# FFT channels of two frequencies in three blocks of 128, two frequency groups, e5m2 transposes and another order of the first loads

## The chip, the cores and the metric

The kernel runs on one core of a Trainium2 chip. The core has five engines, each with a queue of its own that it works through in order: TensorE (PE in the profile, with PEld for its weight loads), VectorE (DVE), ScalarE (ACT), GpSimd (POOL) and SyncE (SP), which here issues all DMAs. The metric is the device time of one execution in microseconds; three runs of the kernel before gave 4522.43, 4522.75 and 4531.9, median 4522.75. The profile is of one further execution, of 4534.8 us by the same clock; the span of its trace is 4533.0 us.

## What is computed

An input of 32 images of 56 x 56 pixels and 96 channels goes through two layers.

- Layer 0 is a convolution block whose weights are mixed per image. The pooled image gives four gates, `rw = sigmoid(pooled @ Wr + br)`; they mix four sets of weights. A pointwise expansion takes 96 to 384 channels, a 3 x 3 depthwise convolution follows, and a pointwise projection takes 384 back to 96. Each has a batch norm, and the input is added.
- Layer 1, first half: every image is a sequence of 3136 tokens. After a layer norm, tokens are projected to 192 channels, and a Fourier transform runs along the 3136 tokens:

```python
h = jax.nn.relu(_bn(jnp.einsum('bnc,hc->bnh', x, w1), ...))
X = jnp.fft.fft(h, axis=1, norm='ortho')
xr = jax.nn.relu(X.real * rd - X.imag * idg + rb)
xi = jax.nn.relu(X.imag * rd + X.real * idg + ib)
y = jnp.fft.ifft(xr + 1j * xi, axis=1, norm='ortho').real
o = jnp.einsum('bnh,ch->bnc', y, w2)
```

  `rd` and `idg` are one number per channel, so the nonlinearity works on each channel and frequency alone.
- Layer 1, second half: layer norm, then two linear layers (96 to 384 to 96) whose operands are rounded to e5m2, an 8-bit float with 5 exponent and 2 mantissa bits.

## The kernel before

An image lies in SBUF as 96 channels by 3136 pixels (`xs[b]`, three buffers). The transform of length 3136 = 56 x 56 is done in two steps of matrix products, with a round trip through DRAM between them. By the names of the tiles:

- `expansion` (tiles `ps_pw`): PE makes 384 channels in three blocks `c` of 128, for each half `p` of the image; ACT evacuates with Relu into the padded tile `hp`. It waits for the mixed weights `wk` of the image. The half p = 1 is computed in 9 + 9 + 8 rows.
- `convolved_tensor` (`ps_dw`) and `convolved_vector` (tile `h`, nine steps): the depthwise convolution, some blocks as 32 x 32 diagonal products on PE, some on DVE.
- `projection` (`ps_pwl`), then `forward(parity)`: transposes and moments of a strip (`ps_t_a`), projection to 192 channels (`ps_w` on `w1c`, evacuated by DVE as `ha`), the first transform step (`ps_a`, evacuated by ACT as `g`), and a write to DRAM (`gd`).
- `frequency_loads` loads groups of the 29 first-step frequencies back into the tile `g2`, called `g` in the profile. `GROUPS` is four groups of 8, 7, 7, 7, and `g2` has two buffers.
- `frequencies` makes the second transform step (`ps_b`): for each group and each half `h` of the 192 channels, one product per frequency, with 96 channels as the stationary (loaded) operand and the 112-column matrix `dftb_s` moving. So the result has 96 channels on partitions.
- `nonlinearity` and `imaginary_parts` work on that result: ACT makes `zi`, `zr` and an absolute value, POOL adds, ACT does a Relu, DVE does four steps that read PSUM or SBUF (tiles `z`, `mir`).
- `spectrum` multiplies by `w2` (`ps_w` on `w_s` and `z`, two products for each frequency, one for each half), ACT copies out (`zo`), `ps_c` makes the first inverse step, DVE copies out, and `zo` goes to DRAM (`yd`).
- `inverse(parity)`: loads a strip `yt`, makes the last inverse step (`ps_d`), adds to the image, transposes (`ps_t_f`), takes moments, normalises on ACT in seven instructions of 96 columns, transposes back (`ps_n`, f32), and runs the two e5m2 layers (`ps_f`; `hidden` between them).

The order of all this is written by a planner when the program is built (class `Plan`). Each step is a generator that yields the engine it wants, the events it waits for and the buffers it takes. The planner keeps a clock per engine with a cost for each instruction (`Engine`, and `mm` for products) and always lets the stream go on that can start first; among equals the smaller priority number wins. The numbers stand in the list at the end of the kernel and in the calls of `plan.spawn`. All PSUM is four buffers of two banks (`ps=4`). When a step on PE gets its buffer and the planner's clock says that PE will stand idle, `psum` puts filler products into the gap, of the size 112 x 112 and at most 40; in the profile they are the lines with L320:

```python
for _ in range(min(40, int((plan.idle() - 0.3) / 0.19))):
    nc.tensor.matmul(ps[:PB, 0:PB], dftb_s, dftb_s, start=True, stop=True)
```

Because the queues are in order, the order that the planner writes is what the chip runs; an engine that is late makes those behind it late.

Ahead of the planned part stands a preparation: loads of all constants by SP, and some 70 small instructions, mostly on DVE, that fold batch norms into the weights. The image loads (`loads`) come after all constants. `mixing` then pools an image on DVE, makes the gates (`ps_rw`, then a sigmoid on ACT with its table load, then four DVE steps for `wk`).

Of the kernel before, what the change touches and what calls it, by code (L numbers as in the profile page):

```python
# [40 lines left out]
F32 = mybir.dt.float32  # L41
# [16 lines left out]
SP64 = 64  # L58
# [20 lines left out]
GROUPS = [(0, 8), (8, 7), (15, 7), (22, 7)]  # L79
# [206 lines left out]
def kernel(  # L286
# [20 lines left out]
    NB = x.shape[0]  # L307

# [14 lines left out]
    plan = None  # L323

# [7 lines left out]

    wpw_s = const([C, NE, M], F32, "wpw_s")
    nc.sync.dma_start(wpw_s, wpw)
    wr_s = const([C, NE], F32, "wr_s")
    nc.sync.dma_start(wr_s, wr)
# [3 lines left out]
    vec_s = const([128, NVECS], F32, "vec_s")  # L340
    nc.sync.dma_start(vec_s, vecs)
# [8 lines left out]
    w2_s = const([C, 2, C], F32, "w2_s")  # L350
    nc.sync.dma_start(w2_s, w2t)
# [11 lines left out]
    nc.vector.tensor_add(ident32, ident32, ident[:, 96:128])  # L363
    ones = const([C, 128], F32, "ones")
# [19 lines left out]
    nid = const([128, 2], F32, "nid")  # L384
    nrd = const([128, 2], F32, "nrd")
# [6 lines left out]
    with tc.tile_pool(name="prep", bufs=1) as pp:  # L392
        row_s = pp.tile([128, NROWS], F32, tag="row_s", name="row_s")
        nc.sync.dma_start(row_s, rows.partition_broadcast(128))

        def row(name, p=128):
            lo, hi = ROWS[name]
            return row_s[:p, lo:hi]

        def bn_scale(to, gamma, var, eps):  # L400

            nc.vector.tensor_scalar_add(to, var, eps)
            nc.scalar.activation(to, to, AF.Sqrt)
            nc.vector.reciprocal(to, to)
            nc.vector.tensor_mul(to, to, gamma)

        bn_scale(s1, vec("g1"), vec("v1"), EPS_CONV)
        bn_scale(s2, vec("g2"), vec("v2"), EPS_CONV)
        bn_scale(s3, vec("g3"), vec("v3"), EPS_CONV)
        bn_scale(sc, vec("cg"), vec("cv"), EPS_ATTN)  # L410
        s1row = pp.tile([C, M], F32, tag="s1row", name="s1row")
        bn_scale(s1row, row("g1", C), row("v1", C), EPS_CONV)
        s3row = pp.tile([128, C], F32, tag="s3row", name="s3row")
        bn_scale(s3row, row("g3"), row("v3"), EPS_CONV)
        sarow = pp.tile([128, CH], F32, tag="sarow", name="sarow")
        bn_scale(sarow, row("ag"), row("av"), EPS_ATTN)
        scrow = pp.tile([C, C], F32, tag="scrow", name="scrow")
        bn_scale(scrow, row("cg", C), row("cv", C), EPS_ATTN)


        for e in range(NE):
            nc.vector.tensor_mul(wpw_s[:, e, :], wpw_s[:, e, :], s1row)
            for c in range(NC3):
                nc.vector.tensor_mul(wpwl_s[:, e, c, :], wpwl_s[:, e, c, :], s3row)
        for h in range(2):
            nc.vector.tensor_mul(w2_s[:, h, :], w2_s[:, h, :], scrow)

        mean_m = pp.tile([C, C], F32, tag="mean_m", name="mean_m")
        nc.gpsimd.memset(mean_m, 1.0 / C)
        center_m = pp.tile([C, C], F32, tag="center_m", name="center_m")  # L430
        nc.vector.tensor_sub(center_m, ident[:C, :C], mean_m)
        nc.vector.tensor_mul(w1c, w1c, sarow[0:C, :])
        ps_c = psum("ps_w1c")
        nc.tensor.matmul(ps_c[:C, 0:CH], center_m, w1c, start=True, stop=True)
        nc.vector.tensor_copy(w1c, ps_c[:C, 0:CH])
        nc.vector.tensor_mul(nshift, row("am"), sarow)
        nc.vector.tensor_sub(nshift, nshift, row("ab"))

        ps_s = psum("ps_shift")
        for h in range(2):  # L440
            nc.tensor.matmul(
                ps_s[:C, 512 * h : 512 * h + 1],
                nshift[0:1, C * h : C * h + C],
                ones[0:1, 0:1],
                start=True,
                stop=True,
            )
        for h in range(2):
            for j, by in enumerate(("rd", "id")):
                nc.vector.scalar_tensor_tensor(  # L450
                    dc[:C, h, j : j + 1], ps_s[:C, 512 * h : 512 * h + 1], -float(S),
                    vec(by)[:C, h : h + 1], ALU.mult, ALU.mult,
                )


        for c in range(NC3):
            taps = stk_s[:, 9 * c : 9 * c + 9, 0:NE]
            nc.vector.tensor_scalar_mul(taps, taps, s2[:, c : c + 1])
            k = 9 * NC3 + c
            nc.vector.tensor_scalar_mul(stk_s[:, k, 0:NE], stk_s[:, k, 0:NE], s1[:, c : c + 1])  # L460
            k += NC3
            nc.vector.tensor_scalar_mul(stk_s[:, k, 0:NE], stk_s[:, k, 0:NE], s2[:, c : c + 1])
        nc.vector.tensor_scalar_mul(stk_s[:, NSTK - 1, 0:NE], stk_s[:, NSTK - 1, 0:NE], s3)
        nc.vector.memset(stk_s[:, 0 : 9 * NC3, NE : NE + 1], 0.0)

        def bn_shift(to, beta, mean, scale, tag):

            tmp = pp.tile(list(mean.shape), F32, tag=tag, name=tag)
            nc.vector.tensor_mul(tmp, mean, scale)
            nc.vector.tensor_sub(to, beta, tmp)  # L470

        k = 9 * NC3
        bn_shift(stk_s[:, k : k + NC3, NE], vec("b1"), vec("m1"), s1, "sh1")
        bn_shift(stk_s[:, k + NC3 : k + 2 * NC3, NE], vec("b2"), vec("m2"), s2, "sh2")
        bn_shift(stk_s[:, NSTK - 1 : NSTK, NE], vec("b3"), vec("m3"), s3, "sh3")
        bn_shift(cb, vec("cb"), vec("cm"), sc, "shc")
        nc.vector.tensor_scalar_mul(nid, vec("id"), -1.0)
        nc.vector.tensor_scalar_mul(nrd, vec("rd"), -1.0)
        nc.vector.tensor_copy(br_s, row("br"))
        for q in range(1, G):  # L480
            for to, at in turned(q):
                nc.sync.dma_start(
                    stk_s[to, NSTK + NPE * (q - 1) : NSTK + NPE * q, :],
                    stk_s[at, 10 * NC3 : 10 * NC3 + NPE, :],
                )


        f1 = pp.tile([C, M], F32, tag="f1", name="f1")
        nc.sync.dma_start(f1, fw1t)
        nc.vector.tensor_copy(fw1, f1, saturate=False)  # L490
        f2 = pp.tile([128, NC3, C], F32, tag="f2", name="f2")
        nc.sync.dma_start(f2, fw2t)
        nc.vector.tensor_copy(fw2, f2, saturate=False)
        q1 = pp.tile([128, NC3], E5M2, tag="q1", name="q1")
        nc.vector.tensor_copy(q1, vec("fb1"), saturate=False)
        nc.vector.tensor_copy(fb1, q1)
        q2 = pp.tile([128, 1], E5M2, tag="q2", name="q2")
        nc.vector.tensor_copy(q2, vec("fb2"), saturate=False)
        nc.vector.tensor_copy(fb2, q2)
# [9 lines left out]
    for t in hp:  # L509
        nc.gpsimd.memset(t, 0.0)  # L510

# [34 lines left out]
    mixed, small_of, wk2s, gds, yds, g2s, zs = {}, {}, {}, {}, {}, {}, {}  # L546


    def loads():
        for b in range(NB):  # L550
            yield SP, [("out", b - 3, s) for s in range(NS) if b >= 3]
            Q.dma_start(xs[b], x[b])
            arrives(4 * C * N, "x", b)
# [71 lines left out]
    def expansion():  # L625

        for b, p, before in parts_of_all():
            xb = xpad[b % 3]
            for c in (2, 0, 1):

                for part, (at, ns) in enumerate(((0, (9, 9)), (18, (8, 8) if p == 0 else (8,)))):
                    yield PE, [("wk", b)] + (readers(*before, c) if before else []), 1
                    wk = mixed[b]
                    ps = psum(f"ps_pw_{b}_{p}_{c}_{part}")
                    for j, n in enumerate(ns):
                        lo = (G * BW * p + at + j * n) * S
                        mm(
                            ps[:, 512 * j : 512 * j + n * S],
                            wk[:, 128 * c : 128 * c + 128],
                            xb[:, lo : lo + n * S],  # L640
                        )
                    plan.spawn("evac pw", 6, expanded(b, p, c, part, at, ns, ps))
# [17 lines left out]
    def convolved_tensor():  # L660

        for b, p, before in parts_of_all():
            for i, wave in enumerate(WAVES[p]):
# [24 lines left out]
                plan.spawn("evac dw", 3, convolved(b, p, i, wave, ps))  # L688
# [41 lines left out]
    def projection():  # L730

        for b, p, _ in parts_of_all():
            needs = [("h2t", b, p, i) for i in range(len(WAVES[p]))] + [("wk2", b)]
            needs += [("h2v", b, p, c) for c, *_ in ON_VECTOR[p]]
            for s, blocks in (((0, (0, 1)), (1, (2, 3))), ((2, (4, 5)), (3, (6,))))[p]:
# [13 lines left out]
                plan.spawn("evac prj", 0, projected(b, s, blocks, ps))  # L749
# [89 lines left out]
    def frequency_loads():  # L839
        n = 0  # L840
        for b in range(NB):
            for i, (k0, nk) in enumerate(GROUPS):
                yield SP, [("g", b, s) for s in range(NS)] + [("g2", n - 2)] * (n >= 2)
                g2 = sp.tile([PB, GK, CH], F32, tag="g2", name=f"g2_{b}_{k0}", bufs=2)
# [4 lines left out]
                g2s[n] = g2  # L849
                arrives(4 * PB * GK * CH, "g2 here", n)  # L850
# [3 lines left out]
    def frequencies():  # L854

        n = 0
        for b in range(NB):
            for i, (k0, nk) in enumerate(GROUPS):
                for h in range(2):
                    yield PE, [("g2 here", n)] + [("z read", n - 2)] * (n >= 2), 1  # L860
# [319 lines left out]
```

## Time and profile before

| | us or share |
|---|---|
| median of three runs | 4522.75 |
| span of the profiled execution | 4533.0 |
| PE busy | 4369.4 (96%) |
| DVE busy | 3598.5 (79%) |
| ACT busy | 2770.5 (61%) |
| POOL busy | 1039.9 (23%) |
| DMA, mean of both kinds of traffic | 75 GB/s |
| DVE steps of the depthwise convolution (`h`) | 1250.1 |
| PE, `ps_dw` | 847.0 |
| PE, `ps_b` | 394.3 |
| PE, `ps_w` on `z` and `w_s` | 398.1 |

A row of the profile's groups reads: line, engine, operation, what is written from what, partitions x elements, count, then busy time and the mean duration of one. An f32 product appears as two records, one behind the other; an f32 transpose and an e5m2 product appear as one. The records of products overlap, because TensorE is pipelined; the time that one costs is the distance from its start to the start of the next. Line 282 is the helper that issues all planned instructions of DVE, ACT, POOL and SP, and line 537 the one that issues products, so the tile names tell what a row is. The page's slices show an even pattern from the second to the last but one: images follow each other in a pipeline, each stage working on another image.

### The profile page before, as it was taken

How to read it: one execution, taken by the hardware profiler on the slowest of the kernel's cores; microseconds unless marked ns; L12 is line 12 of the kernel's file. 1: busy time of each engine (PE TensorE's matmuls, PEld its weight loads, DVE VectorE, ACT ScalarE, POOL GpSimd, SP SyncE). 2: the span in 40 equal slices, each digit the busy share in tenths (PEclk: the TensorE clock that was granted, in tenths of full speed). 3: DMA queues.
4: the chain of work that ended last, by engine and by line, in shares of the span. 5: the costliest groups of instructions: out<-in, count | busy, mean ns of one | idle time of the engine just before them, and what ended most of it. 6: DMA issues, size and time to landing. Idle time of an engine off the chain costs nothing.

```text
span 4533.0 us, 119147 instructions
## 1 busy us (share of the span) xinstructions
PE 4369.4 (96%) x50410; PEld 3236.8 (71%) x50410; DVE 3598.5 (79%) x7474; ACT 2770.5 (61%) x4391; POOL 1039.9 (23%) x1074
## 2 busy tenths in 40 slices
PE   5999999999999999999999999999999999999998
PEld 3667776777776777776777776777776777776778
DVE  4778787788787788787788787788787788787773
ACT  1465666656666656666656666656666656666654
POOL 0012122212122212122212122212122212222212
PEclk9999999999999999999999999999999999999998
DMA  3122332222332223332222322222322222322221
GB/s 89 52 62 64 83 85 77 75 61 78 83 84 78 74 62 78 83 83 78 72 62 80 83 81 81 68 66 79 84 81 81 67 67 77 86 79 83 68 72 45
DMA packets 304494, 339.40 MB, mean 75 GB/s; under 512 B 126836, under 2 KB 243476, under 8 KB 300660
## 3 DMA queue, kind: packets, MB, share of 16 engines
q1 hardware_dynamic: 303960, 331.77, 27.0%
q8 instruction: 397, 6.50, 0.6%
q14 instruction: 137, 1.12, 0.1%
HBM read 163.98 MB, written 158.27 MB: 71 GB/s over the span
## 4 chain that ended last, share of the span: by engine, by line
PE 73%; DVE 13%; ACT 9%; issue 2%; DMA 1%; SPq 0%; POOL 0%; POOLq 0%; ACTq 0%; DVEq 0%
PE ps_dw L537 18%; PE ps_w L537 11%; PE ps_pwl L537 11%; PE ps_pw L537 8%; DVE h L282 7%; PE ps_b L537 6%; PE ps_a L537 5%; ACT h L282 3%; PE ps_f L537 3%; DVE wk L282 3%; PE ps_c L537 3%; PE ps_d L537 2%; ACT mir L282 2%; PE ps_n L541 2%; ACT z L282 2%
## 5 line engine op out<-in xcount | busy, mean ns | idle before, releaser
L282 DVE SCALAR_TENSOR_TENSOR h<-hp,small,h 128x1792 f32<-128x1792 f32 (+2 forms) x768 | 1250.1, 1628 | 23.4 <-ACT h L282 13.7
L537 PE MATMUL ps_dw<-hp,diag 32*32 32x448 f32 x27648 | 847.0, 543 | 0.5 <-ACT mir L282 0.5
L537 PEld LDWEIGHTS ps_dw<-hp,diag 32*32 32x32 f32 x27648 | 541.9, 103 | 247.7 <-issue 72.1
L282 POOL CAST h<-h 128x784 fp8e5<-128x784 f16 x384 | 388.9, 1032 | 800.7 <-DVE h L282 799.1
L537 PE MATMUL ps_pw<-x,wk 96*128 96x504 f32 (+1 forms) x1344 | 571.2, 568 | 0.5 <-DVE ha L282 0.5
L282 ACT ACTIVATE hp<-ps_pw,small 128x1008 f32<-128x1008 f32 (+2 forms) x384 | 362.1, 959 | 295.2 <-DVE wk L282 168.0
L537 PE MATMUL ps_pwl<-h,wk 128*96 128x448 f32 x1344 | 527.3, 540 | 1.9
L282 POOL TENSOR_TENSOR mir<-mir,z 96x392 f32<-96x392 f32 (+1 forms) x256 | 268.9, 1050 | 1007.2 <-ACT mir L282 861.2
L282 ACT ACTIVATE h<-ps_dw,small 128x448 f32<-128x448 f32 x384 | 221.9, 634 | 378.3 <-PE ps_dw L537 378.3
L537 PEld LDWEIGHTS ps_b<-dftb_s,g 112*96 112x96 f32 x3712 | 376.2, 164 | 64.8 <-ACT y L282 30.0
L537 PE MATMUL ps_b<-dftb_s,g 112*96 112x112 f32 x3712 | 394.3, 261 | 28.8 <-ACT y L282 21.1
L282 ACT ACTIVATE z<-ps_b,vec_s 96x392 f32<-96x392 f32 (+1 forms) x512 | 331.6, 687 | 130.4 <-PE ps_b L537 126.5
L537 PEld LDWEIGHTS ps_w<-w_s,z 96*112 96x112 f32 x3712 | 388.4, 181 | 20.9 <-issue 12.6
L537 PEld LDWEIGHTS ps_pw<-x,wk 96*128 96x128 f32 x1344 | 244.3, 190 | 222.5 <-issue 206.4
L537 PE MATMUL ps_w<-w_s,z 96*112 96x96 f32 x3712 | 398.1, 265 | 1.5 <-DVE z L282 1.5
L537 PEld LDWEIGHTS ps_pwl<-h,wk 128*96 128x96 f32 x1344 | 209.7, 163 | 256.7 <-issue 228.5
L282 POOL TENSOR_TENSOR x<-x,y 96x784 f32<-96x784 f32 x128 | 274.4, 2144 | 446.2 <-DVE y L282 429.6
L282 DVE SCALAR_TENSOR_TENSOR ha<-ps_w,rstd_a,nshift 112x192 f32<-112x192 f32 x896 | 312.6, 406 | 77.2 <-PE ps_w L537 77.2
L282 ACT ACTIVATE yt<-yt,nm,rstd_f 112x96 f32<-112x96 f32 x896 | 334.4, 457 | 35.5 <-DVE nm L282 34.9
L537 PE MATMUL ps_a<-ha,dfta_s 112*116 112x192 f32 x1792 | 334.0, 329 | 8.9 <-ACT h L282 8.9
L537 PE MATMUL ps_w<-w1c,x 96*112 96x192 f32 x1792 | 333.0, 329 | 1.5 <-ACT h L282 0.2
L282 DVE SCALAR_TENSOR_TENSOR z<-z,mir 96x392 f32<-96x392 f32 (+1 forms) x512 | 314.0, 662 | 23.7 <-ACT mir L282 23.6
(160 smaller groups left out, 6489.5 us busy)
## 6 DMA issues: line engine op xcount, KB each, us to landing
g<-gd SPq DMA_DIRECT2D x96, 588.0 KB
gd<-g SPq DMA_DIRECT2D x128, 336.0 KB
x<-in_x_dram SPq DMA_DIRECT2D x32, 1176.0 KB
yt<-yd SPq DMA_DIRECT2D x128, 294.0 KB
out_dram<-x SPq DMA_DIRECT2D x128, 294.0 KB
gd<-g SPq DMA_DIRECT2D x128, 252.0 KB
yd<-zo SPq DMA_DIRECT2D x96, 294.0 KB
g<-gd SPq DMA_DIRECT2D x32, 672.0 KB
```

The costliest lines, as they stand in the source:

```text
L282: return getattr(self.namespace, name)(out, *args, **kw)
L537: nc.tensor.matmul(to, lhsT, rhs, start=start, stop=stop)
L541: nc.tensor.transpose(to, ap, eye)
```

## The change

Four things are changed together, with the planner's priorities.

1. *Blocks of 128 channels.* The 192 channels of two neighbouring frequencies are taken as one run of 384 and cut into three blocks of 128 (`NKIND = 3`, "kinds"). Kind 0 is channels 0 to 127 of the first frequency, kind 1 its last 64 and the first 64 of the second, kind 2 the last 128 of the second. `ps_b` then loads 128 columns, and the nonlinearity works on 128 partitions with constants laid out for each kind (`nl_s`). In `spectrum` a pair of frequencies takes three products: one for kind 1 with both frequencies' weights side by side (192 columns moving; rows that belong to the other frequency are zero), and one each for kinds 0 and 2.
2. *Two groups* of 16 and 13 frequencies in place of four. `g2` and `z` have one buffer, so a group's load waits for the products that read the last one. `spectrum` works through a group in pieces of up to eight frequencies.
3. *Transposes of tokens in e5m2.* The normalised strip is written as e5m2 by ACT, and `ps_n` is made by an e5m2 product with an identity in place of an f32 transpose. The value was rounded to e5m2 after the transpose before.
4. *First loads.* Gate weights, image 0 and the rows of constants are loaded first; the blocks of `w2` and of the per-channel constants are loaded by 12 small DMAs. The pool of the preparation is opened earlier.

Also, the second half of the expansion is cut into 8 + 8 + 9 rows, one row less than before.

```diff
-GROUPS = [(0, 8), (8, 7), (15, 7), (22, 7)]
+GROUPS = [(0, 16), (16, 13)]
+NKIND = 3
...
+    wr_s = const([C, NE], F32, "wr_s")
+    nc.sync.dma_start(wr_s, wr)
+    nc.sync.dma_start(xs[0], x[0])
+    prep = tc.tile_pool(name="prep", bufs=1)
+    pp = prep.__enter__()
+    row_s = pp.tile([128, NROWS], F32, tag="row_s", name="row_s")
+    nc.sync.dma_start(row_s, rows.partition_broadcast(128))
     wpw_s = const([C, NE, M], F32, "wpw_s")
...
-    w2_s = const([C, 2, C], F32, "w2_s")
-    nc.sync.dma_start(w2_s, w2t)
+    w2_s = const([128, NKIND, 2, C], F32, "w2_s")
+    nc.gpsimd.memset(w2_s, 0.0)
...
+            nc.sync.dma_start(w2_s[p : p + n, kind, at // CH, :], w2t[c : c + n, h, :])
+            nc.sync.dma_start(nl_s[p : p + n, :, kind], in_vecs[c : c + n, :, h])
...
-                for part, (at, ns) in enumerate(((0, (9, 9)), (18, (8, 8) if p == 0 else (8,)))):
+                for part, (at, ns) in enumerate((((0, (9, 9)), (18, (8, 8))), ((0, (8, 8)), (16, (9,))))[p]):
...
-                yield SP, [("g", b, s) for s in range(NS)] + [("g2", n - 2)] * (n >= 2)
-                g2 = sp.tile([PB, GK, CH], F32, tag="g2", name=f"g2_{b}_{k0}", bufs=2)
+                yield SP, [("g", b, s) for s in range(NS)] + [("g2", n - 1)] * (n >= 1)
...
-                for h in range(2):
-                    yield PE, [("g2 here", n)] + [("z read", n - 2)] * (n >= 2), 1
+                for kind in range(NKIND):
+                    yield PE, [("g2 here", n)] + [("z read", n - 1)] * (n >= 1), 1
...
-                    for k in range(nk):
-                        mm(
-                            ps[:C, 128 * k : 128 * k + PB], g2s[n][:, k, C * h : C * h + C], dftb_s
-                        )
+                    for j in range(size):
+                        at = 2 * CH * j + 128 * kind
+                        mm(ps[:, 128 * j : 128 * j + PB], flat[:, at : at + 128], dftb_s)
...
-        for k in range(nk):
-            for h in range(2):
+        for at in range(0, nk, GK):
...
+            for k in range(0, some, 2):
+                w, j = min(2, some - k), (at + k) // 2
...
+                mm(to, zs[n, 1][:used, j, :], w2_s[:used, 1, 0:w, :], stop=False)
+                for u in range(w):
+                    mm(to[:, u, :], zs[n, 2 * u][:, j, :], w2_s[:, 2 * u, u, :], start=False, stop=u == w - 1)
...
+                nt8 = sp.tile([PB, SQ, C], E5M2, tag=f"nt8{parity}", name=f"nt8_{b}_{s}")
...
-                    transpose(ps[:C, 128 * q : 128 * q + PB], nt[:, q, :], ident[:PB, :PB])
+                    mm(ps[:C, 128 * q : 128 * q + PB], nt8[:, q, :], ident8)
...
-            ("loads", 0, loads()), ("mixing", 7, mixing()), ("inverse", 2, inverse(0)),
-            ("inverse", 2, inverse(1)), ("frequency loads", 5, frequency_loads()),
-            ("frequencies", 3, frequencies()), ("forward", 3, forward(0)),
-            ("forward", 3, forward(1)), ("projection", 5, projection()),
-            ("vector", 4, convolved_vector()), ("tensor", 5, convolved_tensor()),
-            ("expansion", 6, expansion()),
+            ("loads", 0, loads()), ("mixing", 5, mixing()), ("inverse", 3, inverse(0)),
+            ("inverse", 0, inverse(1)), ("frequency loads", 4, frequency_loads()),
+            ("frequencies", 3, frequencies()), ("forward", 2, forward(0)),
+            ("forward", 1, forward(1)), ("projection", 7, projection()),
+            ("vector", 8, convolved_vector()), ("tensor", 6, convolved_tensor()),
+            ("expansion", 9, expansion()),
```

The priorities of the evacuations change too: of `ps_pw` from 6 to 5, of `ps_dw` from 3 to 0, of `ps_pwl` from 0 to 3, of the nonlinearity from 1 to 3, of the spectrum from 2 to 4, and of `hidden` from 3 to 0.

## The prediction

> **What bounds the kernel now.** I read the busy table first, then the chain that ended last, then the waits of TensorE, then one image in order of time.
>
> ```profile
> span 4533.0 us, 119147 instructions
> PE 4369.4 (96%) x50410; PEld 3236.8 (71%) x50410; DVE 3598.5 (79%) x7474; ACT 2770.5 (61%) x4391; POOL 1039.9 (23%) x1074
> PE 73%; DVE 13%; ACT 9%; issue 2%; DMA 1%; SPq 0%; POOL 0%; POOLq 0%; ACTq 0%; DVEq 0%
> ```
>
> TensorE (PE) is busy 96% and holds 73% of the chain. Its waits, longest first:
>
> ```profile
> PE ps_w1c L434 <- DVE w1c L432: 55.9, 1, 55.9
> PE ps_b L537 <- ACT y L282: 21.1, 29, 0.7
> PE ps_w L320 <- DVE z L282: 17.8, 27, 0.7
> PE ps_a L537 <- ACT h L282: 8.9, 30, 0.6
> ```
>
> The first is the start (56 us before any matmul); the others are fractions of a microsecond once an image. Three windows of one image each:
>
> ```profile
> core 0: us, PE busy (x) PEld busy (x) DVE busy (x) ACT busy (x) POOL busy (x), PEclk, DMA share, GB/s
> 1263.20:1399.30 136.10, 133.47 (x1555) 98.43 (x1554) 111.90 (x232) 86.58 (x137) 32.51 (x33) 1.00 0.29 77
> 2217.00:2353.20 136.20, 133.59 (x1568) 98.50 (x1577) 112.01 (x232) 86.58 (x137) 32.57 (x34) 1.00 0.28 76
> ```
>
> An image takes 136.2 us; PE works 133.5 of it, VectorE (DVE) 112, ScalarE (ACT) 87, DMA 0.28. So time is the sum of PE's own instructions, and a change is worth what it does to that sum. But "busy" contains the planner's filler products (line 320), put in where it expects a gap: 28 in each middle image. In order of time, PE alone:
>
> ```profile
> 1320.94 2.85 PE L537 MATMUL ps_b<-dftb_s,g 112*96 112x112 f32 x28
> 1323.62 2.90 PE L537 MATMUL ps_w<-w_s,z 96*112 96x96 f32 x28
> 1326.46 8.79 PE L537 MATMUL ps_dw<-hp,diag 32*32 32x448 f32 x288
> ...
> 1345.55 0.28 PE L537 MATMUL ps_rw<-wr_s,pool_b 96*128 96x4 f32 x2
> ...
> 1354.47 3.70 PE L320 MATMUL ps_pw<-dftb_s 112*112 112x112 f32 x36
> 1358.01 6.57 PE L537 MATMUL ps_pw<-x,wk 96*128 96x504 f32 x16
> ...
> 1376.12 0.84 PE L541 MATMUL ps_n<-ident,yt 112*96 112x112 f32 x7
> 1376.79 0.74 PE L541 MATMUL ps_t_a<-ident,x 96*112 96x96 f32 x7
> ```
>
> Start to next start is the price, since the durations overlap. An f32 product shows as two records. ps_b: 2.68/28 = 95.7 ns a record (112 columns moving, 96 loaded). ps_w with z: the 32 records from 1314.93 to 1318.06 give 97.8, these 28 give 101 (96 moving, 112 loaded); I use 97.8. ps_n: 0.67/7 = 96. Filler: 3.54/36 = 98.3, so 0.197 us a product. In the same view ps_w on w1c (192 moving) takes 1.30/8 = 163.
>
> **What the Trainium skill says.** "TensorE: Matmul & The Clock Gate", section "LDWEIGHTS (loading the stationary operand)": a load takes columns divided by 1.2, whatever the contraction. The trace agrees: ps_w with z moves 96 columns yet takes 97.8 ns, near 112/1.2 = 93. So a product is as dear as the larger of its two sides, and f32 blocks of 128 loaded columns cost more each. Section "Weight-path perf modes — Fast Weight Load (FWL) and DoubleRow": fp8 runs at bf16 speed, and the fast load asks for 128 columns; here 96 are loaded. The trace has fp8 products of 392 columns at 173 ns a record (1271.91 to 1272.95 for six), 0.42 ns a column with 10 ns over, about double the f32 pace.
>
> **The change part by part** (per image, records times ns; counts from the built program).
> 1. ps_b: 58 products of 96 loaded become 44 of 128 loaded. No row shows an f32 load of 128 that bounds; loads of 96, 112, 128 last 163, 178, 190 ns each in the groups, so 12 to 13 more than 112's 97.8, which is bound by its load: 111. Ends: 96 (hidden behind the 112 moving) and 122. 116 x 95.7 = 11.10; 88 x 111 = 9.77: **-1.33** (-2.65 to -0.37).
> 2. ps_w with z: 58 products become 44, 14 of them 192 wide: 116 x 97.8 = 11.35; 28 x 163 + 60 x 97.8 = 10.43: **-0.92**.
> 3. ps_n: 28 f32 transposes become 28 e5m2 products of 112 columns: 112 x 0.42 + 10 = 57, say 60; ends 50 and 85 (96 columns loaded at 1.2). 28 x (97 - 60): **-1.04** (-0.34 to -1.3). The normalisation writes e5m2 instead of f32, same instructions on ACT (457 ns each): nothing.
> 4. The second half of the expansion computes 25 rows, not 26: 3 x 56 columns x 2 / 1.2: **-0.28**.
> 5. ps_c: 8 products, the same columns: 0.
> 6. Fillers: 29 a middle image instead of 28: **+0.2**. Over the program 1383 instead of 1234, counted from one image's first ps_pw to the next: first four stretches 173 instead of 140, twenty-eight middle ones 29 instead of 28, the last, where the pipeline drains, 398 instead of 310.
> Sum in real work: -3.57 x 32 = -114 us. Fillers: 149 more, and 13 fewer of them ahead of the first ps_rw (counted in step 8), so +162 x 0.197 = +32 elsewhere, most of it in the drain, where four frequency steps become two longer ones.
> 7. DVE, ACT and POOL lose a quarter of the nonlinearity: its elements a partition go from 58 x 56 to 44 x 56. DVE spends 642 us there (314 + 163 + 163), ACT 710, so about -4 and -5 us an image. None of it is on the path while PE bounds; it loosens the waits.
> 8. Start. Before, rows landed at 44.4 us and VectorE held everything behind them; 40 fillers (11.1 us from 57.5) then ran past pool_b, ready at 61.5, so ps_rw came at 68.5. After, x of image 0 and the rows go first, but the e5m2 casts of the last loads (fw1, fw2) still stand ahead of the first pooling on VectorE, and SP issues 12 small loads for w2 and the diagonals instead of one, which they pass through. They landed by 46.5; x ahead of them (1176 KB) and the small loads add 6 to 12 us. Pooling then starts about when it did, but only 27 fillers precede ps_rw. I take **-6** (0 to -11).
> 9. Priorities and evacuation order reshuffle all queues; they remove nothing. Their worth is in the waits, 2.6 us an image now. I take no change (-1 to +2). One frequency buffer instead of two: the load of 16 frequencies is 1344 KB; two loads of 1260 KB took from issue at 1291.8 to about 1299.2. From the start of the last ps_a to the first ps_b the new order has 14.4 us of PE work (ps_pwl 4.5, ps_pw 4.7, ps_f 3.1, the rest small). Before, ps_a's start at 1287.3 to the load's end was 11.9; 84 KB more at that pace is 0.5. Hidden, by 2. SP's queue is in order: nothing stands ahead of that load but the writes it needs.
>
> Sum against its own span: 4533 - 114 + 32 - 6 = 4445. The three runs have a median 0.2% under that span (4522.75), so **4437**.
>
> **Rivals.**
> A. *The sum holds*, 4395 to 4475. For: PE waits are small now, every other engine gets less. Against: single buffers.
> B. *New waits give part back*, 4475 to 4513. The new order puts the second group's two halves one behind the other at the end of an image, each with fillers before ps_c (2, 6, 5) because ScalarE must copy zo between. If ACT is later than planned by 0.5 us at each of four places, 32 x 2 = +64: 4500.
> C. *Slower, at one place*: the chain ps_rw, rw on DVE, sigmoid with its table load (1.28 + 0.20), four wk steps (2.35), then the next image's ps_pw. Before, rw stood 4.7 us in DVE's queue, wk was ready 9.8 us after ps_rw, and ps_pw began 12.2 us after: no wait. In the new order only 6.8 us of PE work lie between (21 fillers 4.1, ps_w 1.8, ps_c 0.85). By my count DVE reaches rw 1.3 us after ps_rw: the last z of the second group comes some 6 us after its ps_b, then four steps of 1344 (6.1), the pooling (3.6), a step of 896 (1.1) and zo (0.8), 17.7 in all, while PE needs 16.4 from that ps_b to the end of ps_rw (ps_dw 8.7, ps_w 2.9, two ps_c 2.6, six fillers, ps_a). wk is then ready after 6.0. Should it stand 4.7 us again, PE waits 2.6 an image. The gain of 3.37 an image is gone when rw stands 5.5 us; at 6.5 us the wait is 4.4 and the kernel takes about 4575. What queues behind: ps_d of the older image, so the whole next stretch moves.
> D. *More*, under 4395: weight loads of 128 hide, and DVE's relief removes the present 2.6 us of waits.
> E. *Nothing*: within the 0.2% that measurement of this kernel can tell, by gain and wait cancelling.
>
> **How the numbers follow.** A 0.62, B 0.17, C 0.11, D 0.07, E 0.03. Faster by over 0.2% (under 4513.7): A, B and D, 0.86; same 0.03; slower 0.11. Range: A with nearly all of B, 4395 to 4510.
>
> **What would show it.** ps_b near 111 ns a record over 2816 records, ps_w 163 where wide, ps_n near 60: each read from starts. The period of an image near 133.0 us, DVE near 108 in it. 1383 fillers. ps_rw of the first image near 62. Wrong if the period exceeds 134.5: then look for PE waiting at the first ps_pw of an image (C), at ps_c on zo (B), or at ps_b on the load of g.

## The result and the profile after

The changed kernel takes **4449.43 us** (median; 4436.12 to 4452.19) beside 4523.7 us of the kernel before on the same chip: a ratio of 0.9826, 95% interval 0.9803 to 0.9849. The span of its profiled execution is 4450.0 us, 83.0 less than the 4533.0 of before. Page of the kernel after, first the span, then busy time, then the chain's shares:

```profile
span 4450.0 us, 114927 instructions
PE 4284.4 (96%) x48916; PEld 3152.2 (71%) x48916; DVE 3512.3 (79%) x7222; ACT 2626.6 (59%) x4135; POOL 978.8 (22%) x1012
PE 67%; DVE 13%; ACT 8%; DMA 7%; issue 4%; POOL 1%; SPq 1%; POOLq 0%; ACTq 0%; DVEq 0%
```

PE still bounds, with 85 us less of busy time. But DMA has gone from 1% to 7% of the chain and "issue" from 2% to 4%. Three images of the kernel after, each from one first `ps_dw` to the next (window, its length, then busy us and instructions by engine, the granted clock, DMA share, GB/s):

```profile
core 0: us, PE busy (x) PEld busy (x) DVE busy (x) ACT busy (x) POOL busy (x), PEclk, DMA share, GB/s
1223.24:1362.14 138.90, 132.37 (x1507) 96.16 (x1508) 109.14 (x224) 82.19 (x129) 30.73 (x32) 0.99 0.29 75
1362.14:1494.99 132.85, 129.74 (x1501) 95.04 (x1501) 109.20 (x224) 82.09 (x129) 30.45 (x32) 1.00 0.29 78
1494.99:1627.80 132.81, 130.54 (x1517) 94.87 (x1529) 109.27 (x225) 82.09 (x129) 30.60 (x32) 1.00 0.30 79
```

Two take 132.8 us, the first takes 138.9. Before, the middle images all took 136.1 to 136.9. After, they lie between 132.5 and 138.9 with a median of 133.1 (133.0 was forecast), and about one in three is over 134. Inside an image, PE alone, kernel after (start, duration, what, count; in brackets idle time ahead and what ended it):

```profile
1263.98 1.94 PE L553 MATMUL ps_b<-dftb_s,g 112*128 112x112 f32 x16
1265.75 1.47 PE L553 MATMUL ps_w<-w1c,x 96*112 96x192 f32 x8
...
1285.59 3.02 PE L553 MATMUL ps_w<-w_s,z 128*112 128x192 f32 x24
1288.44 0.74 PE L557 MATMUL ps_t_a<-ident,x 96*112 96x96 f32 x7
1289.02 0.51 PE L553 MATMUL ps_n<-ident,nt 112*96 112x112 fp8e5 x7
1289.37 0.60 PE L321 MATMUL ps_c<-dftb_s 112*112 112x112 f32 x4
```

From start to start, `ps_b` is 1.77/16 = 110.6 ns a record. The piece of `ps_w` with 8 wide and 16 narrow records takes 2.85 us (8 x 163 + 16 x 97.8 would be 2.87). `ps_n` is 0.35/7 = 50 ns. These are the prices of steps 1 to 3. The image of 138.9 us holds this:

```profile
1306.85 4.93 PE L553 MATMUL ps_dw<-hp,diag 32*32 32x448 f32 x152
1312.20 4.04 PE L553 MATMUL ps_dw<-hp,diag 32*32 32x448 f32 x128 [0.42 <-issue]
1319.78 0.95 PE L553 MATMUL ps_dw<-hp,diag 32*32 32x448 f32 x8 [3.55 <-issue]
1320.66 4.72 PE L553 MATMUL ps_w<-w_s,z 128*112 128x192 f32 x24
1325.22 1.36 PE L321 MATMUL ps_c<-dftb_s 112*112 112x112 f32 x12
```

The depthwise products stop twice, for 0.42 and 3.55 us, with no semaphore to wait for ("issue"). Then the same 24 records of `ps_w` take 4.56 us instead of 2.85. Before, 288 such `ps_dw` records ran through in 8.7 us. In windows of 5 us, same columns as above:

```profile
1310.00:1315.00 5.00, 4.58 (x154) 2.51 (x136) 4.93 (x6) 0.00 (x0) 0.00 (x0) 1.00 0.90 228
1315.00:1320.00 5.00, 1.45 (x49) 0.50 (x34) 4.59 (x3) 1.16 (x2) 0.00 (x0) 1.00 0.37 89
1320.00:1325.00 5.00, 5.00 (x30) 4.29 (x23) 1.73 (x2) 2.46 (x3) 0.00 (x0) 0.66 0.01 3
```

DMA is busy 90% in the window ahead of the long stop, and the granted clock is 0.66 in the window after it. The clock records of the trace know only full and half: the 0.66 is half clock for 3.41 us of the 5.

```profile
1320.61:1324.02 3.41, 3.41 (x18) 3.31 (x15) 1.12 (x2) 2.46 (x3) 0.00 (x0) 0.50 0.02 5
```

SyncE's queue and the DMA queue of instructions, first in the kernel after, then in the kernel before:

```profile
1310.44 0.80 SPq L282 DMA_DIRECT2D x<-in_x_dram x1
q8 instruction: 384, 6.29, 0.6%
...
1315.45 0.33 SPq L282 DMA_DIRECT2D x<-in_x_dram x1
q8 instruction: 397, 6.50, 0.6%
```

The load of the next image starts 9.3 us ahead of the second gap's end. TensorE's own instructions come by DMA as well. The Trainium skill ("Runtime: NRT & Kernel Launch", section "Instruction fetch mechanics") says that an engine fetches instructions by DMA in blocks of 256, mostly hidden. The blocks of this queue, 16384 bytes each, are TensorE's: the trace has 48916 products, as many weight loads and 598 records of their sequencer, 98430 in all, which is 384.5 blocks of 256. Before, the same count is 101608, or 396.9 blocks.

The late block can be seen in the trace when these records are numbered in order of time. There are nine gaps of PE between 1.15 and 3.55 us, 22.1 us together, that are put down to "issue" after the start. All nine stand at place 193 or 194 of a block, so any two of them lie a whole number of blocks apart, to within one instruction. Around each, one block's packet is in flight or has just landed, and PE goes on 1.3 to 1.6 us after the end of that packet. From 2 us ahead of the gap to its end, 18 to 66 of the image's 96 rows of 12544 bytes travel beside it. So here the fetch is not hidden: the block comes late while an image is loaded.

Another page ("DMA: Bandwidth & Descriptors", section "Queues, rings and completion order") says that a DMA engine changes queues only between packets, by which it means groups of typically 9 to 17 descriptors, each of which moves one piece. That the block stands behind rows of the image on one DMA engine would follow; the trace does not name the engine that moved a block or a row, so this step is argued and not shown.

A middle image has 3018 instructions of TensorE, 54 short of twelve blocks. The border between two blocks therefore moves by 54 instructions from image to image, and only some images have one in `ps_dw` or just behind it while the load runs. Before, the load was issued 11.0 us ahead of this `ps_dw`, its last row ended 4.4 us ahead of it, and no gap is seen.

The longest waits of PE, kernel after (in all, times, longest):

```profile
PE ps_pw L553 <- DVE z L282: 33.9, 30, 1.4
PE ps_w1c L450 <- DVE w1c L448: 27.1, 1, 27.1
PE ps_rw L553 <- issue: 17.1, 1, 17.1
PE ps_dw L553 <- issue: 14.6, 9, 3.5
PE ps_c L553 <- ACT zo L282: 13.3, 27, 2.0
PE ps_w L553 <- issue: 9.2, 5, 2.7
```

The 21.1 us of `ps_b` on `y` and the 17.8 of a filler on `z` are gone; a wait of about 1.1 us an image ahead of `ps_pw` stands in their place. The start is shorter: the first `ps_pw` begins at 61.25 us instead of 73.99.

### The profile page after: what moved, and what is told of

It is laid out like the page before. It is cut to its first block, busy times and chain, and to the rows that moved or that the text cites. A ratio compares the mean times of both kernels' runs of the same rounds, so it can differ in the third digit from the quotient of the medians.

```text
span 4450.0 us, 114927 instructions
## 1 busy us (share of the span) xinstructions
PE 4284.4 (96%) x48916; PEld 3152.2 (71%) x48916; DVE 3512.3 (79%) x7222; ACT 2626.6 (59%) x4135; POOL 978.8 (22%) x1012
## 4 chain that ended last, share of the span: by engine, by line
PE 67%; DVE 13%; ACT 8%; DMA 7%; issue 4%; POOL 1%; SPq 1%; POOLq 0%; ACTq 0%; DVEq 0%
PE ps_dw L553 14%; PE ps_pwl L553 11%; PE ps_w L553 11%; PE ps_pw L553 8%; PE ps_a L553 5%; DVE h L282 5%; PE ps_b L553 4%; PE ps_f L553 4%; DMA x<-in_x_dram 4%; PE ps_c L553 2%; DMA yd<-zo 2%; ACT z L282 2%; DVE z L282 2%; ACT mir L282 2%; PE ps_t_f L557 2%
## 5 line engine op out<-in xcount | busy, mean ns | idle before, releaser
L553 PE MATMUL ps_pw<-x,wk 96*128 96x448 f32 (+1 forms) x1344 | 571.2, 564 | 34.5 <-DVE z L282 33.9
L282 ACT ACTIVATE hp<-ps_pw,small 128x896 f32<-128x896 f32 (+2 forms) x384 | 361.3, 953 | 268.0 <-PE ps_pw L553 267.7
L282 ACT ACTIVATE nt<-yt,nm,rstd_f 112x96 fp8e5<-112x96 f32 x896 | 334.5, 454 | 201.0 <-DVE nm L282 200.8
L553 PEld LDWEIGHTS ps_w<-w_s,z 128*112 128x112 f32 (+1 forms) x2816 | 361.5, 181 | 56.0 <-issue 48.4
L553 PE MATMUL ps_w<-w_s,z 128*112 128x96 f32 (+2 forms) x2816 | 376.7, 288 | 9.8 <-issue 9.2
L553 PEld LDWEIGHTS ps_b<-dftb_s,g 112*128 112x128 f32 x2816 | 334.8, 192 | 15.9 <-issue 13.2
L553 PE MATMUL ps_b<-dftb_s,g 112*128 112x112 f32 x2816 | 339.0, 274 | 0.0
L553 PEld LDWEIGHTS ps_a<-ha,dfta_s 112*116 112x116 f32 x1792 | 286.0, 181 | 36.5 <-ACT hp L282 31.0
L553 PEld LDWEIGHTS ps_w<-w1c,x 96*112 96x112 f32 x1792 | 284.6, 177 | 37.2 <-ACT h L282 18.9
L282 ACT ACTIVATE z<-ps_b,nl_s 128x448 f32<-128x448 f32 (+2 forms) x384 | 248.7, 689 | 88.3 <-PE ps_b L553 88.0
```

The source lines that it names most:

```text
L282: return getattr(self.namespace, name)(out, *args, **kw)
L553: nc.tensor.matmul(to, lhsT, rhs, start=start, stop=stop)
```

## The experiments

Each ran beside the kernel before; ratios are to it, with 95% intervals. The kernel before took 4525.85 to 4530.67 us beside them, and 4523.7 beside the change, so a difference between the medians of two experiments is uncertain by a few us. "Waits" are the sum over all waits of PE.

**1 and 2. Image loads in four parts.** Same bytes, rows of 3136 bytes instead of 12544, in the changed kernel and in the kernel before:

```diff
-                Q.dma_start(xs[b], x[b])
+                for j in range(4):
+                    Q.dma_start(xs[b][:, j * T : j * T + T], x[b, :, j * T : j * T + T])
```

> The changed kernel with one edit: each image after the first is loaded by four DMAs of 784 pixels a channel (descriptors of 3136 B) instead of one (12544 B). PE's instruction order differs by two filler products. Theory 1, instruction refill: in the changed kernel nine of the long PE gaps (1.2 to 3.6 us each, 'issue' in the waits, and several slow records after them) have one 16384-byte packet of the instruction queue and 4 to 50 packets of 12544 B in flight. If the refill waits on a DMA engine behind the image load, smaller pieces let it in sooner: those gaps fall below 1 us each, 'issue' on ps_dw and ps_w from 24 us to under 8, and the time falls by 25 to 40 us, to 4410 to 4425 (ratio to before 0.975 to 0.978). Rival: the refill is late by itself, whatever else the DMAs carry: no change, ratio 0.982 to 0.984. Third: four issues on SP's queue delay what stands behind them: slower by up to 1.5 us an image.

> The kernel before with the same edit of the image load. Its trace has no 'issue' wait of PE, so theory 1 says no change: ratio 0.998 to 1.002. Rival: the split helps any kernel by quicker loads: ratio under 0.997.

Changed kernel: **4428.1 us**, 0.9784 (0.977 to 0.9797), 21 us under the change as it is (19 by the ratios). Kernel before: 4525.28 us, ratio 1.0 (0.9992 to 1.0008). The change's waits for "issue" in `ps_dw` were halved:

```profile
PE ps_dw L553 <- issue: 7.7, 9, 2.4
```

Those of `ps_w` are gone, and the images now take 132.2 to 136.0 us. The gaps that are left stand at the same place of a block. At the four blocks where the change stops for 3.55, 3.35, 3.27 and 2.73 us in `ps_dw`, this kernel stops for 1.67, not at all, 2.42 and 0.58. All waits of PE fall from 154.1 to 139.8 us, and the time at half clock from 59.8 to 38.1. So the delayed blocks cost about 20 us, less than the 25 to 40 of theory 1, which also expected no gap over 1 us; and they cost it only in the order of the change.

**3. Four parts by channels.** Also four DMAs, but the rows stay 12544 bytes:

```diff
-                Q.dma_start(xs[b], x[b])
+                for j in range(0, C, 24):
+                    Q.dma_start(xs[b][j : j + 24], x[b, j : j + 24])
```

> The changed kernel with each image load in four DMAs of 24 channels, so that there are four DMAs as in the run with four parts of 784 pixels, but every descriptor is still 12544 bytes. Theory 1 (the size of the descriptor ahead of the instruction block decides): nothing is won, 4440 to 4455 us, waits of ps_dw and ps_w called issue about 20 us or more in all. Theory 2 (it is the number of DMAs, since SyncE then hands them over one by one and the queue empties between): 4425 to 4433 us as with the parts of 784 pixels, these waits under 12 us.

4522.37 us, 0.9985 (0.9975 to 0.9994): 73 us above the change, which neither theory had.

```profile
PE ps_rw L553 <- DVE pool_b L282: 62.8, 23, 3.9
...
PE ps_dw L553 <- issue: 12.5, 7, 5.4
PE ps_w L553 <- issue: 10.5, 3, 4.1
PE ps_c L321 <- issue: 3.2, 2, 2.5
PE ps_c L553 <- issue: 0.5, 1, 0.5
```

The waits for issue are 26.7 us, no fewer than the 24.5 of the change, and the longest is 5.4: the number of DMAs alone does not help. What the forecast left out is the load itself. In the middle images it took 8.2 to 11.6 us from the first issue to the end of the last packet, against 6.7 to 9.0 in one DMA and 6.8 to 9.1 in four parts of 784 pixels. So experiment 1's gain does not come from a shorter load, and the size of the rows remains as its likely reason. VectorE's pooling came late here, and PE waited 62.8 us for it instead of 8.8. Why a load of 24 channels is slower was not tried.

**4. The e5m2 transposes alone**, in the kernel before, with its order and its fillers kept:

```diff
...
-                    transpose(ps[:C, 128 * q : 128 * q + PB], nt[:, q, :], ident[:PB, :PB])
+                    plan.tick(PE, 0.083)
+                    nc.tensor.matmul(ps[:C, 128 * q : 128 * q + PB], nt8[:, q, :], ident8, start=True, stop=True)
```

> The kernel before with the token transposes alone made as e5m2 products. The planner is charged the old price for them, so the order and all 1234 fillers stay as they were. ps_n should fall from 96 to about 49 ns a record (as in the changed kernel). If PE's own sum sets the time, 896 x 47 ns = 42 us: about 4481, ratio 0.9905. Rival: where the order stays, what stands behind ps_n waits for ScalarE, which writes n a fixed time after: half of the gain is lost, 4500, ratio 0.995. Zero gain would say that PE is not the bound there.

4504.48 us, 0.9953 (0.994 to 0.9967): 21 us less of the 42 by which the records of `ps_n` differ. The period is 135.3 us instead of 136.2, where 1.34 an image was to be had. Part of the rest became a wait of `ps_f` on ScalarE's `hp`, 12.5 us in 29 images.

**5. The same taken back in the changed kernel** (f32 transposes, its order kept):

```diff
...
-                    mm(ps[:C, 128 * q : 128 * q + PB], nt8[:, q, :], ident8)
+                    plan.tick(PE, 0.051)
+                    nc.tensor.transpose(ps[:C, 128 * q : 128 * q + PB], nt[:, q, :], ident[:PB, :PB])
```

> The changed kernel with the token transposes back in f32, the planner charged the e5m2 price, so that the order and all 1383 fillers stay. ps_n then takes 96 ns a record and not 49: 896 x 47 ns = 42 us if PE's sum alone counts, 4491, ratio 0.993. In the kernel before, the same step was worth 22 us (half), because waits for ScalarE took its place; if that holds here too: 4471, ratio 0.988. Rival: the transposes are hidden in the changed kernel's waits: 4450, ratio 0.983.

4483.81 us, 0.9896 (0.988 to 0.9912): 34 us slower than the change (32 by the ratios), of the 42 by which the records differ. In these two runs, most of what PE is spared reaches the end in the order that was made for it, and about half in the order that was not.

**6. The order of the first loads alone**, in the kernel before:

```diff
+    wr_s = const([C, NE], F32, "wr_s")
+    nc.sync.dma_start(wr_s, wr)
+    nc.sync.dma_start(xs[0], x[0])
...
+    nc.sync.dma_start(row_s, rows.partition_broadcast(128))
...
-            Q.dma_start(xs[b], x[b])
+            if b:
+                Q.dma_start(xs[b], x[b])
```

> The kernel before with the other order of first loads alone: gate weights, image 0 and the rows of constants first; w2 stays one load. From the first expansion on, every engine's order is as before; 1221 fillers, 13 fewer, all ahead of the first ps_rw. My step 8 said -6 us; the traces of the two kernels show the first ps_pw at 74.0 and at 61.3 us, 12.7 apart. Theory A: all of that is the load order: -13 us, ratio 0.9972. Theory B, step 8's size: -6, ratio 0.9987. Theory C: an image at the head of the queue delays the constants and nothing is left: ratio 1.0.

4513.72 us, 0.9966 (0.9953 to 0.9979), which is 15 us less; the first `ps_pw` is at 58.39 us, 15.6 sooner. What the start gains comes through to the end.

**7. No fillers** in the changed kernel; its order stays.

> The changed kernel without any of its 1383 filler products; the order of everything else is the same. In my prediction each counted 0.197 us as if it were work, 272 us in all. Theory A: they stand in gaps that PE has anyway, so the time stays within 15 us of the changed kernel, and waits of about 240 to 272 us appear in their place. Theory B: part of them overshoots the real gap (before ps_pw of the kernel before, the weights were ready 2.3 us ahead of the end of the fillers): faster by 20 to 60 us. Theory C: gaps without them lower the granted clock: slower by 30 us or more, and PE's clock in the page drops below 0.99.

4472.01 us, 0.988 (0.9866 to 0.9893): 23 us slower than with them, though 1383 products are gone. That is theory C, with a little less than its 30 us. Waits of PE in that kernel, and two windows of 10 us:

```profile
PE ps_c L553 <- ACT zo L282: 108.6, 66, 3.5
```

```profile
1320.00:1330.00 10.00, 4.95 (x29) 3.54 (x28) 9.28 (x10) 4.17 (x6) 0.00 (x0) 0.96 0.14 36
1330.00:1340.00 10.00, 9.49 (x19) 4.72 (x20) 8.02 (x13) 3.36 (x4) 2.35 (x3) 0.70 0.32 94
```

PE stands still for half of the first window, at most 3.45 us at a stretch, and then runs on a clock of 0.70; the mean is 0.966 instead of 0.994. The Trainium skill ("TensorE: Matmul & The Clock Gate", section "Part 1: The HAM clock gate (the "warmup" mystery)") says that the clock follows how busy TensorE has lately been, and falls to half after an idle stretch of about 3.4 us. The traces agree that the clock falls to half after idle time, but not on the length: in the change it also fell after single gaps of 2.44, 2.69 and 2.73 us, and experiment 8 shows it fall after waits far shorter. The measurement decides.

**8. The old priorities in the changed kernel, and 9. the new ones in the kernel before.** Only the numbers differ, in this list and in the calls of `plan.spawn`; the planner then writes 1663 and 1976 fillers.

```diff
-            ("loads", 0, loads()), ("mixing", 5, mixing()), ("inverse", 3, inverse(0)),
+            ("loads", 0, loads()), ("mixing", 7, mixing()), ("inverse", 2, inverse(0)),
...
```

> The changed kernel with all planner priorities of the kernel before; work the same, order another. The built program has 1663 fillers, 280 more. If a filler stands for a gap that PE really has, as my count took it: 280 x 0.197 = +55 us: 4504, ratio 0.9957. Rival 1: priorities and the filler count say nothing of the real time: 4450, ratio 0.983. Rival 2: waits that the planner doesn't see come on top: over 4520, ratio above 0.999.

> The kernel before with only the priorities of the change; the planner then writes 1976 filler products instead of 1234. Theory 1 (an order is worth what the planner's fillers say): 742 more by 0.197 us, 4524 + 146 = 4670 us, granted clock near 0.99. Theory 2 (as with the old priorities in the changed kernel, which took 464 us where the fillers said 54: an order that does not fit leaves many short waits of TensorE, and in these the granted clock falls): 4750 us or more, clock under 0.97. Theory 3 (the new priorities are better by themselves and the fillers cover waits that are there anyway): under 4524 us.

**10. Four groups in the changed kernel:**

```diff
-GROUPS = [(0, 16), (16, 13)]
+GROUPS = [(0, 8), (8, 8), (16, 8), (24, 5)]
```

> The changed kernel with four groups of frequencies (8, 8, 8, 5) instead of two, still with one buffer, so that each load waits for the products that read the group before; real work on TensorE differs by one narrow product an image. 1659 fillers instead of 1383. Theory 1 (the groups are worth what the fillers say): 276 by 0.197 us, 4449 + 54 = 4503 us. Theory 2 (the fillers cover waits that the chip does not have, or has in any case): 4445 to 4470 us. Theory 3 (short waits and a lower clock, as with the old priorities): over 4550 us, clock under 0.98.

Measured: 4913.32 us (1.0838, 1.0814 to 1.0861), 4932.57 (1.0899, 1.0879 to 1.0918) and 4814.66 (1.0645, 1.0623 to 1.0667). All are slower by hundreds of microseconds, where the number of fillers said 54 to 146. From the traces, each against the span of the kernel that it was made from (records summed from start to start without gaps):

| | span | fillers | waits of PE | rest: same work, longer records | clock | time at half clock |
|---|---|---|---|---|---|---|
| change without fillers | +16 | -294 | +167 | +142 | 0.966 | +243 |
| change, old priorities | +462 | +60 | +160 | +241 | 0.949 | +446 |
| before, new priorities | +405 | +148 | +160 | +96 | 0.981 | +145 |
| change, four groups | +358 | +71 | +172 | +115 | 0.969 | +240 |

In the three orders of experiments 8 to 10, fillers are 60 to 148 us of 358 to 462; the rest is waits, and the same work done slower. Half of the added time at half clock, 121, 223, 72 and 120 us, is most of that slower work or all of it: an estimate, for work that would have filled this time at full clock. So the forecasts with short waits and a lower clock were right in the time of all three; only the clock of experiment 9, which was to be under 0.97, was 0.981. In the change with the old priorities, PE in order of time:

```profile
1317.24 0.49 PE L553 MATMUL ps_f<-n,fw 96*128 96x392 fp8e5 x2 [0.46 <-ACT n L282]
...
1321.50 2.44 PE L553 MATMUL ps_w<-w1c,x 96*112 96x192 f32 x8 [0.21 <-ACT h L282]
1323.88 3.36 PE L553 MATMUL ps_pw<-x,wk 96*128 96x448 f32 x4
```

Between the first two lines stand five more pairs of `ps_f`, each after 0.21 to 0.22 us of waiting for ScalarE. Then eight records of `ps_w` take 2.38 us instead of 1.31, and four of `ps_pw` 3.15 instead of 1.51; the clock between 1320 and 1330 us is 0.66, with no idle stretch longer than 0.46 us ahead of it. With four groups, the gaps of "issue" in `ps_dw` are 73.1 us in 31 waits; the first seven long ones (2.9 to 3.6 us) each have an instruction block and 44 to 61 rows of the image beside them. Here nearly every image has such a gap, and the count of instructions fits it: an image has 3065 of them, only 7 short of twelve blocks, so a border that falls under the load in one image does so in the next as well. Which of the altered priorities does the harm was not taken apart.

**11 and 12. A better version.** Parts of 784 pixels, and the loads of the two e5m2 layers' weights (`fw1`, `fw2`) put ahead, so that their casts no longer hold VectorE; then also image 1 ahead of `dftd`:

```diff
+    f1 = pp.tile([C, M], F32, tag="f1", name="f1")
+    nc.sync.dma_start(f1, fw1t)
+    f2 = pp.tile([128, NC3, C], F32, tag="f2", name="f2")
+    nc.sync.dma_start(f2, fw2t)
...
-    nc.sync.dma_start(dftd_s, dftd)
...
+    for j in range(4):
+        nc.sync.dma_start(xs[1][:, j * T : j * T + T], x[1, :, j * T : j * T + T])
+    nc.sync.dma_start(dftd_s, dftd)
...
```

> The changed kernel with the image loads in four and two moves among the first loads: the two e5m2 weight loads (fw1, fw2) stand before the big constants, and dftd, which nothing needs in the first 200 us, behind the small copies. In the changed kernel VectorE waited from 31.0 to 48.5 us for fw1, and the first pooling began at 49.8. If that is the start's last wait, pooling begins near 32 and the time falls by some 15 us under the run with the image in four (4428): 4413, ratio 0.975. If the small copies, or w2's loads, then end the wait: -5, 4423, ratio 0.977.

> The kernel of the run before (image loads in four, the two e5m2 layers' weights loaded early), with the load of image 1 put ahead of the table of the last inverse step (dftd), which is needed much later. In that run VectorE waited 18.0 us for image 1, and TensorE then waited 7.1 us for its pooling and 4.6 us for the expansion; the first period was 94.2 us where the changed kernel had 77.1. Theory 1 (these waits are the order of the queue): image 1 lands 6 to 8 us sooner, 6 to 10 us of the 11.7 go, 4414 to 4418 us. Theory 2 (image 1 was held by bandwidth and by images queued with it, not by dftd): less than 3 us, 4421 to 4425.

The first: 4423.9 us, 0.9763 (0.9746 to 0.978). The first `ps_pw` came at 42.59 us, 18.7 sooner, but only 4 us reached the end (10 by the ratios). The time is near the second forecast, but not for its reason: the small copies did not end the wait. VectorE then waited for image 1, still behind `dftd`, and the first period grew by 17.1 us, from 77.1 to 94.2:

```profile
DVE pooled L282 <- DMA x<-in_x_dram: 30.8, 21, 18.0
```

The second: **4416.47 us**, 0.9757 (0.9744 to 0.977), 33 us faster than the change (31 by the ratios) and 110 than the kernel before; the first period is 77.1 us again. By the medians, which come from two chips, the second step is worth 7 us, as in theory 1; by the ratios it is 3, and the two intervals overlap. Its size is open; that the two steps together gain about 12 us over experiment 1 is what both ways of counting say.

## Why the prediction was right

4437 us was forecast and 4449.43 came, inside the range and inside rival A's own. The mechanism held: PE bounds, and the time is near the sum of its instructions and its waits. The steps, over 32 images, from records summed start to start in both traces (us):

| step | forecast | measured |
|---|---|---|
| 1 `ps_b` | -43 | -50 |
| 2 `ps_w` with z | -29 | -24 (-32 in experiment 1) |
| 3 `ps_n` | -33 | -42 |
| 4 one row less | -9 | -5 |
| 6 fillers | +32 | +39 |
| 8 start | -6 | -13 |
| 9 waits of PE outside the start | 0 | +16 |
| `ps_f`, same instructions | 0 | -17 |
| `ps_dw`, same instructions | 0 | +12 |
| sum | -88 | -84 (spans: -83) |

The three rows above the sum stood at nothing in the forecast and came out at +16, -17 and +12. That they nearly cancel is luck, and so is part of the nearness of the sum; why `ps_f` became cheaper was not tried. Start and fillers overlap by some 1 us. Steps 1 and 2, the largest, were not run by themselves: their worth is read from the records alone, while experiments 4 to 6 took steps 3 and 8 apart.

- Steps 1 and 2: 110.6 ns and 163/97.8 as worked out. A load of 128 columns bounds, as taken from the durations of the loads. `ps_b` gained more than the -43, since its records before cost 97.9 ns on the mean of the whole trace and not 95.7.
- Step 3 was mis-sized: 50 ns, not 60. I had put the lower end at 50 and taken a cautious value between; the upper end of 85, where a load of 96 columns bounds, is not seen.
- Step 5: `ps_c`, forecast unchanged, went from 158 to 162 us. Step 7: DVE, forecast near 108 us in an image, shows 109.2; that relief is off the path.
- Step 8 was half of the truth. I let the pooling wait for the casts of `fw1` and `fw2`, which it did (VectorE idle for 17.3 us before the first cast), but expected these loads 6 to 12 us later than the 46.5 of before: the first landed at 48.5 us, and the gate came at 53.84 and not near 62. The 13 us are outside the step's own range of 0 to 11. Experiment 6 gets 15 us from that order alone.
- Step 9 had the mechanism wrong, without tipping the sum. It said that the new order moves waits and removes nothing, worth -1 to +2 us an image, and the measured +16 us are 0.5 an image, inside that range. But it missed a resource: the moved load of the image meets TensorE's own instruction blocks, 22.1 us of gaps and slower records behind them. Experiment 1 gives about 20 us of it back; experiment 2 shows that smaller rows gain nothing in the kernel before.
- Of the rivals, B named the wrong place: `ps_c` on `zo` waits 13.3 us in all, not 64. C did not come: no wait of an image's first `ps_pw` for `wk` is among those shown. The new wait ahead of `ps_pw`, 33.9 us, was in no rival and takes the place of the two that went.
- Costing the order at nothing came out right only because the order fits this kernel. Experiments 8 to 10 show how far a price by fillers can miss: an order made by other priorities cost 400 us more.

## What to carry over

Where one engine is busy 96% of the time, price its records from start to start. Here that came within 0.3%, with errors that partly cancelled. Beside it, look at what each moved DMA will run next to: in this kernel a stretch of many short instructions needed its instruction blocks from DMA too, and they came late beside large rows of another load; smaller rows gave back about 20 us. Gaps that always lie a whole number of 256 instructions apart are the sign of it. An order written out by a planner fitted one kernel and cost the other hundreds of microseconds: short waits cost twice here, once as waits and again through the clock.

## Not expected of the hardware

- Instruction blocks of 16384 bytes arrived late beside image rows of 12544 bytes: gaps of 1.15 to 3.55 us, all at one place of a block of 256 instructions, and up to 5.4 us with loads of 24 channels. With rows of 3136 bytes the longest was 2.4 us, and about 20 us came back.
- After a gap of 3.55 us the granted clock was half for 3.41 us, and 24 records took 4.56 us instead of 2.85. Seven waits of 0.2 to 0.5 us in a row were followed by half clock for 6.83 us.
- An e5m2 product of 112 columns with 96 loaded costs 50 ns, an f32 product with 128 loaded and 112 moving 110.6 ns a record.
- Four DMAs of 24 channels took 8.2 to 11.6 us for an image that one DMA of 96 channels brought in 6.7 to 9.0.
